# Layer 0's selective scan: dt and u are spread over the partitions by transfers from DRAM instead of by TensorE's products

## The chip, the cores and the metric

The kernel runs on one core of one Trainium2 chip. The metric is the device time of one execution, in microseconds (us); less is better. Of the kernel before there are three runs, with a median of 7452.86 us (7450.63 to 7460.66), and one execution under the hardware profiler.

The core has five engines with instruction streams of their own: TensorE (PE, matrix products, with PEld for its weight loads), VectorE (DVE), ScalarE (ACT), GpSimd (POOL) and SyncE (SP), which here only issues DMA transfers. They meet through semaphores. SBUF is the working memory of 128 partitions; PSUM, of eight banks of 512 float32 columns in each partition, takes TensorE's results, and DVE and ACT can read and write it. Transfers are carried out by 16 DMA engines.

## What is computed

Four residual layers work on x of 8 images, 128 channels and 64x64 pixels, float32. The change is in layer 0, in a selective state-space scan over the 4096 pixels of an image, with 128 inner channels d and N = 16 states n:

```python
dbc = xc @ xproj_w
dt = softplus(dbc[..., :R] @ dt_w + dt_b)
Bm = dbc[..., R:R + N]
Cm = dbc[..., R + N:]
A = -exp(A_log)
dA = exp(dt[..., None] * A)
dBx = dt[..., None] * Bm[:, :, None, :] * xc[..., None]
# step: h = dA_t * h + dBx_t ;  y_t = sum over n of h * C_t
```

So each of 128 x 16 pairs (d, n) has a recurrence of its own along the pixels. The decay is exp(dt[d] A[d, n]), the input u[d] B[n] with u = dt xc, and the output is weighed by C[n] and summed over n. Layer 0 further has a group norm, a small projection t, a layer norm, a convolution of three taps along the pixels, gates, and a 3x3 convolution of the other 64 channels. Layer 1 is a recurrence over image rows and then columns, of convolutions with nine taps; layers 2 and 3 follow.

## The kernel before

**Tiles and steps.** `layer0` works through 32 chunks of 1024 pixels, four an image; a chunk is two halves h of T = 512 pixels. The 2048 recurrences of a half are 16 rows of 128, since 128 partitions hold 8 channels with 16 states each. A *step* takes two of these rows: 8 steps a half, 16 a chunk, 512 in all. `where(i)` gives the chunk, the half, and (r, j0): the step's rows are the channels 32 j + 8 r to 32 j + 8 r + 7 for j = j0 and j0 + 1.

**What a step does.** `step_dt` (through `spread`, L571 to L580) multiplies 32 rows of dt by a mask `m_dt` that holds A at (d, n) and zeros elsewhere: PE so copies each channel to its 16 partitions and scales it by A, into `dt_ps` in PSUM. `step_decay` (L592) takes the exponential of both rows in one ACT instruction, into `da`. `step_u` does the same as `step_dt` for u with the mask `m_u` of ones, into `u_ps`. `step_scan` multiplies `u_ps` by B on DVE, in place (L599), and runs two scans, one for each row, into `hb` (L610); `carry` gives the start values. `step_carry` and `step_weigh` on POOL keep the last column (L616) and multiply `hb` by C (L621). Every second step, `round_sum` sums over n with a mask on PE (L629), into `ps_y`.

**What a chunk does once.** `plan_chunk` puts some 30 pieces of work at ticks relative to t0 = 16 c: load and norm of x, the product for t (L362) and its variance, products for x and z (`xs_product`, L392; `z_product`, L404), the softplus for dt in pieces from `v_product` to `v_sum`, and after the scan `y_gate`, `y_mul`, the 3x3 convolution (L484), `y_product` and the stores. `v_sum` (L439 to L441) makes dt and u with three POOL operations a half, into SBUF. `bc_product` writes B and C to a small DRAM tile `bcd`, and `bc_spread` (L457) loads them back, eight transfers a half of 16 partitions each, so that each partition has its n's row of B and C in one tile `bc`.

**What sets the order.** The order is written out by hand: the loop at L645 to L662 issues, for tick i, the scan of step i, layer 1's addition, u of step i + 1, dt of step i + 2, the sum of i - 3, the decay of i + 2, carry and weighing of i - 1, then the chunk pieces of tick i, and last layer 1's products. Each engine, SyncE among them, executes its own part of that order strictly in sequence; semaphore waits follow from the tiles. All of layer 0's transfers are issued by SyncE.

**Layer 1 inside layer 0.** From tick 294 on `Layer1First` adds one row of layer 1's recurrence to each tick, for the first four images: 18 matmul instructions (L739) at the end of a tick, and one DVE operation (L747) at the next. It needs 252 ticks and goes on for 34 after the last scan. Its PSUM bank is the second of two `u_ps` pairs, which layer 0 gives up at tick 280.

**PSUM of layer 0:** two `u_ps` of two banks, `dt_ps` of two banks, one bank for `ps_y` and one (`ps_g`) for all products of the chunk pieces.

Of the kernel before, what the change touches and what calls it, by code (L numbers as in the profile page):

```python
# [10 lines left out]
F32 = mybir.dt.float32  # L11
I32 = mybir.dt.int32
AF = mybir.ActivationFunctionType
ALU = mybir.AluOpType
# [3 lines left out]
P = 128  # L18
# [16 lines left out]
def conv_preact_kernel(ctx: ExitStack, tc: tile.TileContext, a: dict, out: bass.AP):  # L35
# [31 lines left out]
    bcd = [dram.tile([P // 2, T], F32, name=f"bcd{i}") for i in range(2)]  # L67
# [12 lines left out]
    layer0(tc, a, ident, gmat, x_in, x1d, bcd, norm1, Layer1First(tc, a, w1, x1d, norm1, X))  # L80
# [67 lines left out]
def layer0(tc, a, ident, gmat, x_in, x1d, bcd, norm1, layer1):  # L148
# [5 lines left out]
    nc = tc.nc  # L154
    CH = 2 * T
    CR = CH // W
    NCK = HW // CH
    with ExitStack() as ctx:
# [3 lines left out]

        pu = ctx.enter_context(tc.tile_pool(name="l0u", bufs=1, space=PSUM))
        pdt = ctx.enter_context(tc.tile_pool(name="l0dt", bufs=1, space=PSUM))
        py = ctx.enter_context(tc.tile_pool(name="l0y", bufs=1, space=PSUM))
        pg = ctx.enter_context(tc.tile_pool(name="l0g", bufs=1, space=PSUM))
# [25 lines left out]
        a_neg = load("a_neg", [DI, N], (ALL, a["A_log"]))  # L192
# [4 lines left out]
        with tc.manual_schedule():  # L197
# [5 lines left out]
            def ps_g(name):  # L203
                return pg.tile([P, T], F32, tag="g", name=name)
# [47 lines left out]
            quad = wp.tile([P, 32], F32, name="quad")  # L252
            nc.vector.tensor_copy(quad, ident[:, 0:32])
            for j in range(1, 4):
                nc.vector.tensor_add(quad, quad, ident[:, 32 * j : 32 * j + 32])
            m_u = wp.tile([P, 4, 8, N], F32, name="m_u")
            nc.vector.tensor_copy(
                m_u, quad.rearrange("p (r d) -> p r d", d=8).unsqueeze(3).to_broadcast([P, 4, 8, N])
            )
            m_dt = wp.tile([P, 4, 8, N], F32, name="m_dt")  # L260
            nc.vector.tensor_mul(
                m_dt, m_u, a_neg.unsqueeze(1).unsqueeze(1).to_broadcast([P, 4, 8, N])
            )
# [70 lines left out]

            def plan_chunk(c):
# [50 lines left out]
                def xs_product(h):  # L386
                    q, sl = s["q"], (LO, HI)[h]
                    if h == 0:
                        s["xz"] = w2.tile([DI, 6, T], F32, name="xz", bufs=1)
                    ps = ps_g("ps_x")  # L390
                    for k in range(KC):
                        nc.tensor.matmul(  # L392
                            ps, lhsT=w_k[sl, k, :], rhs=q[sl, k : k + T], start=(k == 0), stop=(k == KC - 1)
                        )
                    edge = KC - 1 if g == 0 and h == 0 else 0
                    x = s["xz"][:, h]
                    nc.scalar.activation(x[:, edge:], ps[:, edge:], AF.Identity, bias=b_xc[:, 2:3])
                    for i in range(edge):
                        nc.scalar.activation(x[:, i : i + 1], ps[:, i : i + 1], AF.Identity, bias=b_xc[:, i : i + 1])

                def z_product(h):
                    q, sl = s["q"], (LO, HI)[h]
                    ps = ps_g("ps_z")
                    nc.tensor.matmul(ps, lhsT=in_w[sl, DI:], rhs=q[sl, KC - 1 :], start=True, stop=True)  # L404
                    nc.scalar.activation(s["xz"][:, 2 + h], ps, AF.Identity, bias=in_b[:, 1:2])
# [29 lines left out]
                def v_sum(h):  # L435
                    dt = s["dt", h] = w2.tile([DI, T], F32, name=f"dt{h}", bufs=1)
                    u = s["u", h] = w2.tile([DI, T], F32, name=f"u{h}", bufs=1)
                    w = s["w"][:, h]
                    nc.gpsimd.tensor_add(w, w, s["e"][:, h])  # L439
                    nc.gpsimd.tensor_add(dt, w, s["rv"][:, h])  # L440
                    nc.gpsimd.tensor_mul(u, dt, s["xc"][:, h])  # L441
# [12 lines left out]
                def bc_spread(h):  # L454
                    bc = s["bc", h] = w2.tile([P, 2, T], F32, name="bc")
                    for d in range(8):
                        nc.sync.dma_start(  # L457
                            bc[16 * d : 16 * d + 16],
                            bcd[c % 2][32 * h : 32 * h + 32, :].rearrange("(i n) t -> n i t", n=N),
                        )  # L460
# [72 lines left out]
                at(t0 - 25, t_product)  # L533
                at(t0 - 24, t_var)
# [3 lines left out]
                at(t0 - 21, t_norm)  # L538
                at(t0 - 19, t_edge)
                for h in range(2):  # L540
                    at(t0 - 16 + h, also(xs_product, h))
                    at(t0 - 14 + h, also(z_product, h))
                    at(t0 - 11 + h, also(v_product, h))
                    at(t0 - 6 + 4 * h, also(v_sum, h))
                    at(t0 - 6 + 8 * h, also(bc_spread, h))
                    at(t0 + 10 + 8 * h, also(y_gate, h))
                    at(t0 + 11 + 8 * h, also(y_mul, h))
                at(t0 - 13, silu)
                at(t0 - 9, bc_product)
                at(t0 - 10, v_exp)  # L550
                at(t0 - 9, v_round)
                at(t0 - 8, v_rest)
                at(t0 - 7, v_log)
# [17 lines left out]
            def spread(i, ps, mask, src):  # L571
                c, h, r, j0 = where(i)
                for j in (0, 1):
                    q = slice(32 * (j0 + j), 32 * (j0 + j) + 32)
                    nc.tensor.matmul(  # L575
                        ps[:, j, :],
                        lhsT=mask[q, r].rearrange("p d n -> p (d n)"),
                        rhs=S[c][src, h][q, :],
                        start=True, stop=True,
                    )  # L580

            def step_u(i):
                steps[i]["bc"] = u_ps[0 if i > shared else i % 2]
                spread(i, steps[i]["bc"], m_u, "u")

            def step_dt(i):
                steps[i] = {"dt": pdt.tile([P, 2, T], F32, name="dt_ps")}
                spread(i, steps[i]["dt"], m_dt, "dt")

            def step_decay(i):  # L590
                da = steps[i]["da"] = w2.tile([P, 2, T], F32, name="da", bufs=3)
                nc.scalar.activation(da, steps[i]["dt"], AF.Exp)  # L592

            def step_scan(i):
                c, h, r, j0 = where(i)
                s, st = S[c], steps[i]
                if r == 0 and j0 == 0:
                    s["carry", h] = w2.tile([P, 4, 4], F32, name="carry")
                nc.vector.tensor_mul(  # L599
                    st["bc"], st["bc"], s["bc", h][:, 0].unsqueeze(1).to_broadcast([P, 2, T])  # L600
                )
                hb = st["hb"] = w2.tile([P, 2, T], F32, name="hb", bufs=4)
                for j in (0, 1):
                    if h:
                        start = s["carry", 0][:, r, j0 + j : j0 + j + 1]
                    elif c % NCK:
                        start = S[c - 1]["carry", 1][:, r, j0 + j : j0 + j + 1]
                    else:
                        start = 0.0
                    nc.vector.tensor_tensor_scan(  # L610
                        hb[:, j, :], st["da"][:, j, :], st["bc"][:, j, :], start, ALU.mult, ALU.add
                    )
# [5 lines left out]
            def step_weigh(i):  # L618
                c, h, r, j0 = where(i)
                hb = steps[i]["hb"]  # L620
                nc.gpsimd.tensor_mul(hb, hb, S[c]["bc", h][:, 1].unsqueeze(1).to_broadcast([P, 2, T]))  # L621
# [15 lines left out]

            shared = n_steps // 2 + 24
            u_ps = [pu.tile([P, 2, T], F32, name=f"u_ps{i}") for i in range(2)]
            layer1.begin(16 * NCK, shared, u_ps[1])  # L640
# [4 lines left out]
            for i in range(min(events), n_steps + 60):  # L645
                if 0 <= i < n_steps:
                    step_scan(i)
                layer1.add(i)
                if 0 <= i + 1 < n_steps:
                    step_u(i + 1)  # L650
                if 0 <= i + 2 < n_steps:
                    step_dt(i + 2)
                if i % 2 and 0 <= i - 3 < n_steps:
                    round_sum(i - 3)
                if 0 <= i + 2 < n_steps:
                    step_decay(i + 2)
                if 0 <= i - 1 < n_steps:
                    step_carry(i - 1)
                    step_weigh(i - 1)
                for what in events.pop(i, ()):  # L660
                    what()
                layer1.products(i)  # L662
# [9 lines left out]
class Layer1First:  # L672
# [5 lines left out]
    def begin(self, batch, first, bank):  # L678

        ps = bank[:, 0, 0 : W * NB2].rearrange("p (w b) -> p w b", b=NB2)  # L680
        self.steps = propagate(self.tc, self.a, self.wp, ps, self.X)
        self.batch, self.first = batch, first + 14
# [601 lines left out]
def layouts(i):  # L1284
# [20 lines left out]
        "A_log": i["L0_conv_A_log"],  # L1305
# [34 lines left out]
```

## Time and profile before

| | before |
|---|---|
| median of three runs | 7452.86 us |
| the profiled execution | 7436.8 us |
| its span | 7435.1 us |
| PE busy | 5633.9 us, 76% |
| DVE busy | 4822.2 us, 65% |
| POOL busy | 4120.9 us, 55% |
| ACT busy | 3349.0 us, 45% |
| moved by DMA | 935.09 MB, mean 126 GB/s |
| first scan; first product of layer 1; last scan | 96.9; 1445.6; 2955.8 us |

In the page's groups a line has the source line, the engine and the operation, what is written and read, the count, then busy time and mean duration of one, and last the idle time of the engine just before with what ended most of it. In a table by stretch a row has the stretch and its length, then for each engine the busy time and, in brackets, the number of instructions, the granted share of TensorE's clock, the mean busy share of the 16 DMA engines, and what they moved. A line of a timeline has start and length, the engine and the source line. fp32 products appear as two PE instructions each.

### The profile page before, as it was taken

To read this page: it belongs to the slowest core of one execution; us is meant where nothing else is said; L and a number is where in the kernel's file an instruction comes from. 1 tells how busy PE (TensorE), PEld (TensorE's weight loads), DVE (VectorE), ACT (ScalarE), POOL (GpSimd) and SP (SyncE) were. 2 spreads that over 40 slices of the span, in tenths; PEclk is the share of its full clock that TensorE was granted. 3 is DMA by queue.
4 is the path that set the end of the run, shared out by engine and by line. 5 is a ranking of instruction groups with operands and counts; after the bars stand their busy time and mean duration, and the time that the engine had idled before them with its cause. 6 is when DMAs were issued, how large, how long until landed. Compare 5 with 4: busy or idle time off the path is not lost.

```text
span 7435.1 us, 79753 instructions
## 1 busy us (share of the span) xinstructions
PE 5633.9 (76%) x25130; PEld 3374.0 (45%) x25130; DVE 4822.2 (65%) x6334; ACT 3349.0 (45%) x7610; POOL 4120.9 (55%) x3773
## 2 busy tenths in 40 slices
PE   6888888899999999779898988984556565554330
PEld 1222222255556556647676767762333333333220
DVE  4988889666666666230366666758767676776665
ACT  3555655433333332020255555554556565565552
POOL 3878778545545454000255555555666666666664
PEclk9888888799999999989999999996777677776665
DMA  1111111101100100130356666667677666666667
GB/s 57 43 58 54 57 56 53 42 29 34 32 30 30 31 20 18 59 124 24 96 180 188 189 183 180 192 187 243 211 217 219 208 212 209 211 212 201 187 182 272
DMA packets 360134, 935.09 MB, mean 126 GB/s; under 512 B 64168, under 2 KB 99248, under 8 KB 357664
## 3 DMA queue, kind: packets, MB, share of 16 engines
q0 software_dynamic: 184320, 604.13, 26.7%
q1 hardware_dynamic: 170784, 309.09, 12.8%
q10 hardware_dynamic: 4608, 16.78, 0.6%
q8 instruction: 200, 3.28, 0.2%
q14 instruction: 222, 1.82, 0.1%
HBM read 804.35 MB, written 125.40 MB: 125 GB/s over the span
## 4 chain that ended last, share of the span: by engine, by line
PE 56%; ACT 11%; issue 9%; DVE 9%; another core or an unknown queue 7%; DMA 4%; POOL 4%; SPq 0%; POOLq 0%; DVEq 0%; ACTq 0%
PE u_ps L739 13%; PE ps_l L739 11%; ACT X L1184 6%; PE u_ps L575 5%; PE ps_o L1227 5%; PE ps_c L484 3%; PE ps_t L900 3%; PE ps_y L629 3%; PE ps_s L1209 2%; PE ps_x L392 2%; DVE hb L610 2%; POOL hb L621 2%; PE ps_off L1017 2%; PE ps_t L926 1%
## 5 line engine op out<-in xcount | busy, mean ns | idle before, releaser
L1173 POOL DMA_INDIRECT X<-table,idx x1386 | 1317.9, 951 | 717.0 <-issue 276.6
L1173 POOL DMA_INDIRECT got<-table,idx x918 | 885.1, 964 | 1291.2 <-DVE idx L1078 529.6
L621 POOL TENSOR_TENSOR hb<-hb,bc 128x1024 f32<-128x1024 f32 x512 | 1207.1, 2358 | 47.0 <-POOL carry L616 4.5
L610 DVE TENSOR_TENSOR_SCAN hb<-da,carry,u_ps 128x512 f32<-128x512 f32 x896 | 1097.8, 1267 | 76.4 <-PE ps_y L629 19.8
L592 ACT ACTIVATE da<-dt_ps 128x1024 f32<-128x1024 f32 x512 | 524.8, 1025 | 1284.2 <-PE dt_ps L575 1087.4
L1184 ACT ACTIVATE X<-X,wgt 128x128 f32<-128x128 f32 x2772 | 867.5, 396 | 41.5 <-issue 37.7
L1227 PE MATMUL ps_o<-samp,dcn_w 128*128 128x256 f32 x2304 | 711.8, 455 | 182.9 <-issue 95.8
L1219 ACT COPY samp<-ps_s 128x384 f32<-128x384 f32 x768 | 362.9, 473 | 1043.9 <-remote 563.0
L575 PE MATMUL u_ps<-u,m_u 32*128 32x512 f32 x2048 | 652.3, 716 | 131.2 <-DVE hb L610 130.5
L599 DVE TENSOR_TENSOR u_ps<-u_ps,bc 128x1024 f32<-128x1024 f32 x512 | 625.8, 1222 | 191.2 <-PE dt_ps L575 173.9
L1209 PE MATMUL ps_s<-ident,X 128*128 128x128 f32 x1386 | 306.4, 344 | 576.2 <-ACT samp L1219 287.0
L575 PE MATMUL dt_ps<-dt,m_dt 32*128 32x512 f32 x2048 | 664.0, 728 | 31.5 <-ACT da L592 25.7
L1227 PEld LDWEIGHTS ps_o<-samp,dcn_w 128*128 128x128 f32 x2304 | 507.3, 231 | 309.4 <-issue 128.6
L747 DVE SCALAR_TENSOR_TENSOR X<-ps_l,X 128x256 f32<-128x256 f32 x252 | 106.6, 423 | 734.5 <-PE ps_l L739 553.6
L1200 DVE TENSOR_TENSOR prod<-prod,X 128x384 f32<-128x384 f32 x462 | 260.8, 565 | 480.0 <-ACT X L1184 320.5
L1184 ACT ACTIVATE got<-got,wgt 128x128 f32<-128x128 f32 x1836 | 570.3, 393 | 1.1 <-issue 1.1
L1209 PEld LDWEIGHTS ps_s<-ident,X 128*128 128x128 f32 x1386 | 206.1, 176 | 708.9 <-ACT samp L1219 330.5
L616 POOL COPY carry<-hb 128x2 f32<-128x2 f32 x512 | 111.4, 218 | 735.0 <-DVE hb L610 678.8
L1189 DVE TENSOR_TENSOR prod<-X,prod 128x768 f32<-128x768 f32 x462 | 444.5, 962 | 46.2 <-ACT prod L1156 27.6
L747 DVE SCALAR_TENSOR_TENSOR X<-u_ps,X 128x256 f32<-128x256 f32 x252 | 106.9, 424 | 562.7 <-PE u_ps L739 560.4
L900 PE MATMUL ps_t<-xn,w 128*128 128x512 f32 (+4 forms) x688 | 344.8, 656 | 66.5 <-issue 23.0
L575 PEld LDWEIGHTS u_ps<-u,m_u 32*128 32x128 f32 x2048 | 169.6, 202 | 483.6 <-DVE hb L610 282.2
(227 smaller groups left out, 10644.6 us busy)
## 6 DMA issues: line engine op xcount, KB each, us to landing
bc<-bcd SPq DMA_DIRECT2D x512, 64.0 KB
table<-tok SPq DMA_DIRECT2D x128, 256.0 KB
x<-x1d SPq DMA_DIRECT2D x96, 256.0 KB
X<-table,idx POOLq DMA_INDIRECT x1386
x<-x2d SPq DMA_DIRECT2D x48, 384.0 KB
x3h<-x3d SPq DMA_DIRECT2D x16, 1056.0 KB
x_st<-in_x SPq DMA_DIRECT2D x64, 256.0 KB
x_o<-in_x SPq DMA_DIRECT2D x64, 256.0 KB
```

The source lines that it names most:

```text
L575: nc.tensor.matmul(ps[:, j, :], lhsT=mask[q, r].rearrange("p d n -> p (d n)"), rhs=S[c][src, h][q, :], start=True, stop=True,)
L592: nc.scalar.activation(da, steps[i]["dt"], AF.Exp)
L599: nc.vector.tensor_mul(st["bc"], st["bc"], s["bc", h][:, 0].unsqueeze(1).to_broadcast([P, 2, T]))
L610: nc.vector.tensor_tensor_scan(hb[:, j, :], st["da"][:, j, :], st["bc"][:, j, :], start, ALU.mult, ALU.add)
L621: nc.gpsimd.tensor_mul(hb, hb, S[c]["bc", h][:, 1].unsqueeze(1).to_broadcast([P, 2, T]))
L739: nc.tensor.matmul(ps[:, c0:c1, :], lhsT=w[:, k, :], rhs=v[:, prev, c0 + k - PAD : c1 + k - PAD, :], start=(k == PAD), stop=(k == K - 1),)
L900: nc.tensor.matmul(ps[:, o0 - a0 : o1 - a0, :], lhsT=self.w1[:, k, :], rhs=S["xn", g][:, i0 + o0 : i0 + o1, :], start=(k == 2), stop=(k == 4),
L1173: nc.gpsimd.indirect_dma_start(out=got[:, k, :, :].rearrange("p q c -> p (q c)"), out_offset=None, in_=tab, in_offset=bass.IndirectOffsetO ...
L1184: nc.scalar.activation(got[:, k, q, :], got[:, k, q, :], AF.Identity, scale=wgt[:, t, k0 + k, q : q + 1])
L1189: nc.vector.tensor_mul(prod, got[:, :, 0:2, :], w.unsqueeze(3).to_broadcast([P, G3, 2, C]))
L1209: nc.tensor.transpose(ps[:, k, :], got[:, k, 0, :], self.ident)
L1227: nc.tensor.matmul(ps, lhsT=self.dcn_w[:, k, :], rhs=samp[:, k - k0, :], start=(k == 0), stop=(k == KK - 1))
```

## The change

dt and u no longer go through PE.

- `v_sum` stores both to DRAM with the new `keep`, eight transfers a chunk, of 64 rows by 512 columns each. In DRAM the rows are ordered (a, r, d, j), so that the two rows j of a channel that belong to one step are next to each other.
- `step_dt` and `step_u` are now one transfer each: 8 channels of 2 x 512 floats, each read for 16 partitions (`to_broadcast`), straight into `da` and `hb`. They are issued four and three steps ahead; `da` has five buffers instead of three and `hb` six instead of four.
- A is no longer in a mask. `a_neg` is reshaped to 16 columns by 128 partitions, and `step_decay` gives a column as `scale` to ACT: two instructions of 128x512, in place in SBUF, instead of one of 128x1024 from PSUM.
- `bc_spread` is one transfer for B and one for C a half, with a leading broadcast of 8. B goes to a tile that shares the buffer `tcen`, and `b_copy` on ACT moves it to PSUM. The product u B reads `hb` and B and writes a PSUM tile of its own (`ps_ub`); the scans write `hb` as before.
- In PSUM now: two banks for `ps_ub`, two for B, one for `ps_y`, one for layer 1, two for the chunk products. With two of these, `xs_product` and `z_product` do both halves in one tick, with the halves' instructions in turn, and `v_product` does both at one tick.
- The pieces of the chunk before the scan move one tick earlier in part (`t_product` to `t_edge`, and `v_product` to `v_sum`). Layer 1 begins at tick 294 as before.

```diff
@@ layer0: PSUM pools
         pu = ctx.enter_context(tc.tile_pool(name="l0u", bufs=1, space=PSUM))
-        pdt = ctx.enter_context(tc.tile_pool(name="l0dt", bufs=1, space=PSUM))
+        pb = ctx.enter_context(tc.tile_pool(name="l0b", bufs=2, space=PSUM))
         py = ctx.enter_context(tc.tile_pool(name="l0y", bufs=1, space=PSUM))
-        pg = ctx.enter_context(tc.tile_pool(name="l0g", bufs=1, space=PSUM))
+        pl = ctx.enter_context(tc.tile_pool(name="l01", bufs=1, space=PSUM))
+        pg = ctx.enter_context(tc.tile_pool(name="l0g", bufs=2, space=PSUM))
...
-        a_neg = load("a_neg", [DI, N], (ALL, a["A_log"]))
+        a_neg = load("a_neg", [P, 4, 4], (ALL, a["A_log"]))
...
+            def keep(d, t):
+                d = d.rearrange("(a r d j) t -> a j (r d) t", a=2, r=4, j=2)
+                for a in range(2):
+                    nc.sync.dma_start(d[a], t[64 * a : 64 * a + 64])
...
-                def xs_product(h):
...
+                def xs_product():
+                    s["xz"] = w2.tile([DI, 6, T], F32, name="xz", bufs=1)
+                    pss = [ps_g("ps_x") for _ in range(2)]
                     for k in range(KC):
+                        for ps, sl in zip(pss, (LO, HI)):
+                            nc.tensor.matmul(
+                                ps, lhsT=w_k[sl, k, :], rhs=s["q"][sl, k : k + T],
+                                start=(k == 0), stop=(k == KC - 1),
+                            )
...
                 def v_sum(h):
-                    dt = s["dt", h] = w2.tile([DI, T], F32, name=f"dt{h}", bufs=1)
-                    u = s["u", h] = w2.tile([DI, T], F32, name=f"u{h}", bufs=1)
-                    w = s["w"][:, h]
+                    w, dt = s["w"][:, h], s["rv"][:, h]
                     nc.gpsimd.tensor_add(w, w, s["e"][:, h])
-                    nc.gpsimd.tensor_add(dt, w, s["rv"][:, h])
-                    nc.gpsimd.tensor_mul(u, dt, s["xc"][:, h])
+                    nc.gpsimd.tensor_add(dt, w, dt)
+                    keep(dtu[c % 2][h][0], dt)
+                    nc.gpsimd.tensor_mul(w, dt, s["xc"][:, h])
+                    keep(dtu[c % 2][h][1], w)
...
                 def bc_spread(h):
-                    bc = s["bc", h] = w2.tile([P, 2, T], F32, name="bc")
-                    for d in range(8):
-                        nc.sync.dma_start(
-                            bc[16 * d : 16 * d + 16],
-                            bcd[c % 2][32 * h : 32 * h + 32, :].rearrange("(i n) t -> n i t", n=N),
-                        )
+                    b_in = s["b_in"] = w2.tile([P, T], F32, tag="tcen", name="b_in", bufs=1)
+                    s["C", h] = w2.tile([P, T], F32, name="C")
+                    for i, t in enumerate((b_in, s["C", h])):
+                        at = 32 * h + N * i
+                        nc.sync.dma_start(t, bcd[c % 2][at : at + N, :].unsqueeze(0).to_broadcast([8, N, T]))
+
+                def b_copy(h):
+                    s["B", h] = pb.tile([P, T], F32, name="ps_b")
+                    nc.scalar.copy(s["B", h], s["b_in"])
...
-            def spread(i, ps, mask, src):
+            def spread(i, k, t):
                 c, h, r, j0 = where(i)
+                src = dtu[c % 2][h][k].rearrange("(a r d j) t -> a r d (j t)", a=2, r=4, j=2)[j0 // 2, r]
+                nc.sync.dma_start(t.rearrange("p j t -> p (j t)"), src.unsqueeze(1).to_broadcast([8, N, 2 * T]))
+
+            def step_dt(i):
+                steps[i] = {"da": w2.tile([P, 2, T], F32, name="da", bufs=5)}
+                spread(i, 0, steps[i]["da"])
+
+            def step_u(i):
+                steps[i]["hb"] = w2.tile([P, 2, T], F32, name="hb", bufs=6)
+                spread(i, 1, steps[i]["hb"])
+
+            def step_decay(i):
+                _, _, r, j0 = where(i)
+                da = steps[i]["da"]
                 for j in (0, 1):
-                    q = slice(32 * (j0 + j), 32 * (j0 + j) + 32)
-                    nc.tensor.matmul(
-                        ps[:, j, :],
-                        lhsT=mask[q, r].rearrange("p d n -> p (d n)"),
-                        rhs=S[c][src, h][q, :],
-                        start=True, stop=True,
-                    )
...
+                    nc.scalar.activation(da[:, j], da[:, j], AF.Exp, scale=a_neg[:, r, j0 + j : j0 + j + 1])
...
-                nc.vector.tensor_mul(
-                    st["bc"], st["bc"], s["bc", h][:, 0].unsqueeze(1).to_broadcast([P, 2, T])
-                )
-                hb = st["hb"] = w2.tile([P, 2, T], F32, name="hb", bufs=4)
+                hb = st["hb"]
+                ub = pu.tile([P, 2, T], F32, name="ps_ub")
+                nc.vector.tensor_mul(ub, hb, s["B", h].unsqueeze(1).to_broadcast([P, 2, T]))
...
@@ the loop over ticks
-                if 0 <= i + 1 < n_steps:
-                    step_u(i + 1)
-                if 0 <= i + 2 < n_steps:
-                    step_dt(i + 2)
+                if 0 <= i + 4 < n_steps:
+                    step_dt(i + 4)
                 if i % 2 and 0 <= i - 3 < n_steps:
                     round_sum(i - 3)
+                if 0 <= i + 3 < n_steps:
+                    step_u(i + 3)
                 if 0 <= i + 2 < n_steps:
                     step_decay(i + 2)
```

## The prediction

> **What bounds the kernel now.** I read the page, then busy time by stretch, then groups, chain and timeline inside the stretches, last the DMA. All the change touches runs from the first scan (93 us) to the last (2958 us): 512 steps. Layer 1's first products are at 1445 us, step 294, so there are two stages. Busy time by stretch:
>
> ```profile
> core 0: us, PE busy (x) PEld busy (x) DVE busy (x) ACT busy (x) POOL busy (x), PEclk, DMA share, GB/s
> 93.00:1445.00 1352.00, 1127.85 (x4925) 294.08 (x4924) 1169.75 (x1082) 721.71 (x847) 1050.80 (x815) 0.83 0.17 52
> 1445.00:2960.00 1515.00, 1497.30 (x7490) 904.12 (x7491) 967.48 (x988) 483.42 (x564) 764.58 (x594) 0.99 0.09 28
> 2960.00:3127.00 167.00, 145.89 (x658) 118.41 (x658) 20.57 (x47) 7.08 (x9) 7.56 (x7) 1.00 0.04 14
> ```
>
> Stage 1 takes 1352/294 = 4.60 us a step; DVE is busy 1170/294 = 3.98 of them and PE 3.84, each waiting for the other in turn. Stage 2 takes 1515/218 = 6.95 us a step and is PE's, at 99%. DMA is idle five sixths of the time. Work of a step, from the page's groups:
>
> ```profile
> L621 POOL TENSOR_TENSOR hb<-hb,bc 128x1024 f32<-128x1024 f32 x512 | 1207.1, 2358 | 47.0 <-POOL carry L616 4.5
> L610 DVE TENSOR_TENSOR_SCAN hb<-da,carry,u_ps 128x512 f32<-128x512 f32 x896 | 1097.8, 1267 | 76.4 <-PE ps_y L629 19.8
> L592 ACT ACTIVATE da<-dt_ps 128x1024 f32<-128x1024 f32 x512 | 524.8, 1025 | 1284.2 <-PE dt_ps L575 1087.4
> L599 DVE TENSOR_TENSOR u_ps<-u_ps,bc 128x1024 f32<-128x1024 f32 x512 | 625.8, 1222 | 191.2 <-PE dt_ps L575 173.9
> ```
>
> The chain of stage 2, in order of time, shows what the removed products cost there: they run in pairs, u beside dt, from 2202.46 to 2203.53, that is 1.07 us a step.
>
> ```profile
> 2202.46 0.63 PE u_ps L575 x2
> 2203.09 0.01 PE dt_ps L575 x2
> 2203.10 0.41 PE u_ps L575 x2
> 2203.51 0.01 PE dt_ps L575 x2
> 2203.53 1.00 PE ps_y L629 x8
> 2204.52 2.77 PE ps_x L392 x6
> ```
>
> The DMA answer for 300 to 1300 us (14 chunks): SyncE's queue, then the issues that the change replaces.
>
> ```profile
> q1 hardware_dynamic: 30016, 53.93, 17.2%
> ...
> bc<-bcd SPq DMA_DIRECT2D x224, 64.0 KB
> ```
>
> And SyncE's timeline in layer 2, where two stores of 67 rows (L869) are followed by three of 64 rows:
>
> ```profile
> 3692.83 0.68 SPq L869 DMA_DIRECT2D table<-zero  x2
> 3693.55 7.88 SPq L871 DMA_DIRECT2D table<-zero  x3
> ```
>
> Issuing those three takes 7.88 us, where three ordinary issues take about 1.3. The packet records behind it show the 67-row stores' 2048-byte packets one after another, one each 80 ns: a single engine works on them.
>
> [...] packets of 2048 bytes last 86 ns in the store of 128 partitions (L513) and 151 in that of 64 (L452). [...]
>
> **The change, part by part.**
>
> PE loses eight product records a step, 1.07 us in stage 2 and some 2.0 in stage 1 (1010.56 to 1012.58 us, at a lower clock). `xs_product` and `z_product` now alternate halves of the rows, as u and dt did, so a second half costs about nothing: 2.77 + 1.05 = 3.8 us a chunk, 0.24 a step. PE would need 6.95 - 1.07 - 0.24 = 5.64 us a step in stage 2.
>
> ACT: `step_decay` becomes two exponentials of 128x512. The nearest row is L305's from SBUF, 626 ns: 1.25 us for 1.02. `b_copy` adds two of about 0.58 a chunk. ACT was busy 2.45 us a step and becomes 2.75; the period hides it, and it would cost 0.3 a step without cover. DVE and POOL do the same work: 3.98 and 3.57 us. The removed masks and the reshaped A are before the loop.
>
> DMA, of a chunk of 16 steps. `step_dt` and `step_u`: 32 transfers of 512 KB, 16.8 MB where the whole queue carried 53.93/14 = 3.9. The source is 8 rows x 16 repeats x 4096 bytes[...]. Packets of 4096 bytes last 159 ns (the median in the records, at the end of the kernel). 32 x 16 x 159 ns = 81.4 us[...]. `bc_spread`: four of 8 x 16 rows[...]: 4 x 16 x 84 ns = 5.4. `keep`: eight stores of 64 rows into (2, 32) rows[...]: 8 x 32 packets[...]: 151 ns, 38.7 us; 86 ns, 22.0[...]. What stays: 17.2% of 1000 us over 14 chunks is 12.3 us, less L457's 32 packets an engine at 0.101, 3.2: 9.1.
>
> Engine 0: 81.4 + 5.4 + 9.1 + 22.0 to 38.7 = 118 to 135 us a chunk, 7.4 to 8.4 us a step. That is more than either stage's period: DMA becomes the bound of both, and what PE gives up is worth nothing. [...] (151/86 = 1.76) [...] (81.4 + 5.4) x 1.76 + 9.1 = 162 us, 10.1 a step. [...] I take the middle, 8.75[...].
>
> SyncE: dt of step i+4 waits for the scan of i-1 (five `da`), u of i+3 for `round_sum(i-3)` (six `hb`). Behind them stand `keep`, `bc_spread`, image loads and output stores. When scan i-1 has run, u of i+1 and i+2 and dt of i+2 and i+3 are still queued, over 10 us of transfers, so these waits don't empty the engines. `keep` must land before its half's first dt, three steps later, some 26 us: enough, unless stores queue behind more. `b_in` shares `tcen` with `t_norm`, a step earlier: hidden. At the start `keep` comes ahead of the first scan: +15 us.
>
> Sum: 512 x 8.75 = 4480, before 1352 + 1515 = 2867: +1613, +15. Span 7435.1 + 1628 = 9063, the execution 1.7 more; the median of the runs (7452.86) stands 16 above the profiled execution (7436.8), so 9080 us.
>
> **The rivals.**
>
> All sixteen engines serve the transfers[...]. Then 32 x 8 x 159 ns + 2.7 + 5 + 9.1 is 57.5 us a chunk, 3.6 a step, hidden. Stage 1 falls to DVE's 3.98 and some 0.17 of gaps, 4.15: -132; stage 2 to 5.64: -286. 7453 - 418 = 7035. For it: the idle DMA above, and that the waits of DVE and ACT are all for PE. Against it: the 67 rows. This decides for faster where the busiest engine needs less than 2867/512 = 5.6 us a step.
>
> The spreads use sixteen but `keep` two: 40.7 + 2.7 + 38.7 + 9.1 = 91 us, 5.7 a step; stage 1 +323, stage 2 -272: 7500. [...]
>
> [...] 10.1 a step: 5171 - 2867 + 15 = +2319, 9770. It is the forecast's own upper end.
>
> **How the numbers follow.** Eight engines, 7.4 to 10.1 us a step: 0.83, with its own range 8390 (512 x 7.4 - 2867 + 15 on 7453) to 9770. Sixteen throughout: 0.10. Only `keep` narrow: 0.04. Slower still[...]: 0.03. The three runs span 0.13%, so under 0.2% nothing can be told. Range 8200 to 10000: it leaves out the faster cases, most of the slowest, and a few in a hundred of the forecast by a cheaper `keep`. Faster 0.11, same 0.01, slower 0.88.
>
> **What would show it.** The DMA share near one half in both stages (eight full engines of sixteen), never near 0.8; stages of nearly equal step time, so stage 1 longer by far more than stage 2; DVE and ACT waiting for `da` and `hb` by DMA; PE busy far under 99% in stage 2; scan, weighing and product at 1.27, 2.36 and 1.22 us. It is wrong if the share passes 0.6 at a step of 5.6 us or less, if DVE's product slows, or if SyncE's waits, not the packets, fill the gaps.

## The result, and the profile after

The changed kernel took 8477.57 us (median of four runs, 8469.99 to 8495.37) where the kernel before took 7456.76 beside it (7450.63 to 7467.47): a ratio of 1.137, 95% interval 1.135 to 1.139. The forecast was 9080 with a range of 8200 to 10000, so the direction and the range were right and the value was 600 us too high. The profiled span is 8468.3 us, against 7435.1.

Busy time by stretch, with the columns of the table shown for before: stage 1 (first scan to layer 1's first product), stage 2 (to the last scan), and the rest of layer 1's first half.

```profile
98.00:2316.00 2218.00, 997.15 (x2546) 229.59 (x2548) 1198.39 (x1080) 816.91 (x1175) 1047.96 (x808) 0.55 0.50 180
2316.00:3957.00 1641.00, 1326.94 (x5741) 883.69 (x5738) 950.53 (x988) 553.64 (x806) 767.78 (x594) 0.90 0.48 173
3957.00:4135.00 178.00, 151.45 (x680) 122.12 (x679) 27.58 (x56) 7.07 (x9) 10.10 (x9) 0.98 0.06 20
```

Both stages now run at one pace: from scan to scan 7.54 us a step in stage 1 (before 4.57) and 7.56 in stage 2 (6.98). Stage 1 is 873 us longer, stage 2 126, and the first scan comes 2 us later: 1001 of the span's 1033 us. The other 32 lie behind the last scan, in code that was not touched; in the pair of traces taken later on one chip they are absent (there the last scan is 996 us later and the span 994 longer). None of PE, DVE, ACT and POOL is full any more: PE is busy for 45% of stage 1 and 81% of stage 2, DVE for 54 and 58. The DMA share stands at one half in both stages, which is what eight engines of sixteen, nearly full, would look like.

The page's groups, for the same four pieces of a step as before, in the order POOL, DVE, ACT, DVE:

```profile
L624 POOL TENSOR_TENSOR hb<-hb,C 128x1024 f32<-128x1024 f32 x512 | 1208.4, 2360 | 41.3 <-POOL carry L619 0.6
L613 DVE TENSOR_TENSOR_SCAN hb<-da,carry,ps_ub 128x512 f32<-128x512 f32 x896 | 1098.3, 1268 | 81.8 <-DVE ps_ub L605 58.1
L596 ACT ACTIVATE da<-da,a_neg 128x512 f32<-128x512 f32 x1024 | 681.2, 712 | 2129.0 <-DMA da<-dtd 2045.8
L605 DVE TENSOR_TENSOR ps_ub<-hb,ps_b 128x1024 f32<-128x1024 f32 x512 | 628.8, 1228 | 1450.5 <-DMA hb<-ud 1448.6
```

The weighing (2360 ns for 2358), the scan (1268 for 1267) and DVE's product (1228 for 1222) cost what they did. What changed is the last column: ACT stands 2046 us for `da` by DMA, and DVE 1449 us for `hb` by DMA, where both waited for PE before. The waits of 300 to 2300 us say the same; the columns are the total, the number of waits and the longest, in us:

```profile
ACT da L596 <- DMA da<-dtd: 969.3, 188, 15.1
DVE ps_ub L605 <- DMA hb<-ud: 848.3, 246, 14.1
```

SyncE's queue and the two new transfers, from the page's parts on DMA:

```profile
q1 hardware_dynamic: 319776, 879.52, 29.4%
...
da<-dtd SPq DMA_DIRECT2D x512, 512.0 KB
hb<-ud SPq DMA_DIRECT2D x512, 512.0 KB
```

And SyncE's timeline for one stretch of stage 1:

```profile
1249.00 3.62 SPq L331 DMA_DIRECT2D dtd<-xz  x2
1252.72 5.12 SPq L331 DMA_DIRECT2D ud<-xz  x2
1257.96 5.73 SPq L582 DMA_DIRECT2D da<-dtd  x1
1263.79 1.18 SPq L582 DMA_DIRECT2D hb<-ud  x1
```

An issue that takes some 0.53 us in a run below takes up to 5.73 here, and SyncE is issuing for 69% of stage 1. Two readings fit: the engines that serve the queue are short, or SyncE itself has become the bound. The experiments start there. (The chain that ended last can't be used: its traced pieces lie behind layer 1.)

### The profile page after: what moved, and what is told of

It is laid out like the page before. It is cut to its first block, busy times and chain, and to the rows that moved or that the text cites. A ratio compares the mean times of both kernels' runs of the same rounds, so it can differ in the third digit from the quotient of the medians.

```text
span 8468.3 us, 75234 instructions
## 1 busy us (share of the span) xinstructions
PE 5330.0 (63%) x21034; PEld 3291.6 (39%) x21034; DVE 4830.3 (57%) x6328; ACT 3510.8 (41%) x8186; POOL 4120.5 (49%) x3773
## 5 line engine op out<-in xcount | busy, mean ns | idle before, releaser
L596 ACT ACTIVATE da<-da,a_neg 128x512 f32<-128x512 f32 x1024 | 681.2, 712 | 2129.0 <-DMA da<-dtd 2045.8
L605 DVE TENSOR_TENSOR ps_ub<-hb,ps_b 128x1024 f32<-128x1024 f32 x512 | 628.8, 1228 | 1450.5 <-DMA hb<-ud 1448.6
L624 POOL TENSOR_TENSOR hb<-hb,C 128x1024 f32<-128x1024 f32 x512 | 1208.4, 2360 | 41.3 <-POOL carry L619 0.6
L613 DVE TENSOR_TENSOR_SCAN hb<-da,carry,ps_ub 128x512 f32<-128x512 f32 x896 | 1098.3, 1268 | 81.8 <-DVE ps_ub L605 58.1
L632 PE MATMUL ps_y<-hb,m_y 128*32 128x512 f32 x2048 | 451.6, 810 | 593.2 <-POOL carry L619 392.1
L739 PE MATMUL ps_l<-X,w_right 128*128 128x256 f32 x2268 | 540.0, 396 | 125.6 <-DVE X L747 83.5
L739 PE MATMUL ps_l<-X,w_left 128*128 128x256 f32 x2268 | 537.1, 394 | 121.0 <-DVE X L747 81.8
L739 PE MATMUL ps_l<-X,w_up 128*128 128x256 f32 x2268 | 537.5, 394 | 101.8 <-DVE X L747 74.8
L739 PE MATMUL ps_l<-X,w_down 128*128 128x256 f32 x2268 | 530.5, 390 | 78.9 <-DVE X L747 77.4
L739 PEld LDWEIGHTS ps_l<-X,w_right 128*128 128x128 f32 x2268 | 448.9, 202 | 234.5 <-DVE X L747 117.7
```

The lines of the kernel that those rows point to most:

```text
L596: nc.scalar.activation(da[:, j], da[:, j], AF.Exp, scale=a_neg[:, r, j0 + j : j0 + j + 1])
L605: nc.vector.tensor_mul(ub, hb, s["B", h].unsqueeze(1).to_broadcast([P, 2, T]))
L613: nc.vector.tensor_tensor_scan(hb[:, j, :], st["da"][:, j, :], ub[:, j, :], start, ALU.mult, ALU.add)
L624: nc.gpsimd.tensor_mul(hb, hb, S[c]["C", h].unsqueeze(1).to_broadcast([P, 2, T]))
L632: nc.tensor.matmul(S[c]["ps_y", h][32 * j : 32 * j + 32, :], lhsT=m_y[:, r, :], rhs=steps[i + j // 2]["hb"][:, j % 2, :], start=(r == 0), ...
L739: nc.tensor.matmul(ps[:, c0:c1, :], lhsT=w[:, k, :], rhs=v[:, prev, c0 + k - PAD : c1 + k - PAD, :], start=(k == PAD), stop=(k == K - 1),)
```

## The experiments

They ran on several chips. On most of them the unchanged layers behind layer 1's first half are faster: the kernel before takes 7000 us there, but in the trace taken there its two stages are the same. So ratios and stages are compared, not totals; the totals expected of the first three edits are on the scale of the first chip, where the kernel before takes 7457. "A step" is the time from scan to scan; packet times are means over the records of the 4096-byte packets in stage 1. Each ratio has several runs behind it, each step time one trace.

**The two kernels on one chip.**

> The changed kernel again, on the chip of the other experiments, for its ratio and its stages there. All theories: stages of 7.5 and 7.6 us a step as in the first run, some 1020 us over the kernel before (7003 here), so a ratio near 1.145.

> The kernel before, for a trace on the chip of the experiments. Stages of 4.57 and 6.98 us a step as on the first chip; what follows layer 1's first half near 3890 us, as in the other runs on this chip, instead of 4312.

Ratio 1.144 (1.142 to 1.146); steps of 7.53 and 7.55 us after, 4.57 and 6.98 before. What follows layer 1's first half takes 3881 and 3884 us. So the whole loss is in the two stages.

**n outermost.** The partitions of a step are ordered (n, d), so the source of a spread is 16 repeats of 8 rows; B and C are spread in the same order. Bytes and number of issues stay; only what stands outermost changes.

```diff
- src.unsqueeze(1).to_broadcast([8, N, 2 * T])
+ src.unsqueeze(0).to_broadcast([N, 8, 2 * T])
```

> Partitions in the order (n, d) instead of (d, n), so that the broadcast source of da, hb, B and C has 16 rows outermost. Theory 1, the busiest DMA engine sets the step: these transfers run on 16 engines instead of 8, engine 0 has 43 + 9 + 22 to 39 us a chunk, 4.7 to 5.7 us a step; stage 1 near 4.9 us a step, stage 2 at PE's 5.6 to 5.8, time 7200 to 7450. Theory 2, SyncE's issues and waits set the step, not the engines: the same number of issues, so 8300 to 8500, no change. Theory 3, only the stores of dt and u on two engines bind: 8000 to 8400, since they stay.

Ratio 1.038 (1.037 to 1.040), steps of 6.02 and 6.23 us. That is the direction of theory 1, but not the 4.9 and 5.6 to 5.8 us a step that it named.

**`keep` over sixteen engines.** Its eight stores of (2, 32) rows a chunk become sixteen of 32 rows.

```diff
- nc.sync.dma_start(d[a], t[64 * a : 64 * a + 64])
+ for j in range(2):
+     nc.sync.dma_start(d[a, j], t[64 * a + 32 * j : 64 * a + 32 * j + 32])
```

> Each store of 64 rows is cut in two of 32 rows with 32 outermost, so that it runs on 16 engines; the spreads stay on 8. Theory 1: engine 0 loses the stores, some 20 us of 120.6 a chunk, and is as loaded as engines 1 to 7: 6.0 to 6.5 us a step, 7700 to 7950. Theory 2: eight more issues a chunk, 0.5 us each: 8500 to 8650. Theory 3: down to the periods of the compute engines, under 7400.

Ratio 1.172 (1.169 to 1.175), steps of 7.82 and 7.91 us. In the two stages that is 164 us more than the changed kernel, so some 8640 on the first chip: the number of theory 2, at the edge of its range, and far from theory 1. But it is not theory 2's cause: SyncE issues for 53% of stage 1 where it did for 69%, and the packets below show full engines.

**Both edits.**

> Both edits. Theory 1: at most 60 us a chunk on any engine, 3.7 us a step, hidden: stage 1 at DVE's 4.15 us a step, stage 2 at PE's 5.64, 7035 (6980 to 7200), faster than the kernel before. Theory 2: 8500 or more. Theory 3: as with the stores alone.

Ratio 1.011 (1.010 to 1.013), steps of 5.52 and 6.04 us, far from the 4.15 and 5.64 of theory 1. The stretch from 300 to 1300 us, in the run with n outermost, with `keep` alone and with both:

```profile
300.00:1300.00 1000.00, 554.92 (x1454) 129.61 (x1451) 678.59 (x610) 466.26 (x671) 597.95 (x463) 0.57 0.89 226
```

```profile
300.00:1300.00 1000.00, 446.61 (x1118) 101.79 (x1120) 512.95 (x464) 343.06 (x497) 454.55 (x351) 0.53 0.56 170
```

```profile
300.00:1300.00 1000.00, 592.13 (x1586) 136.56 (x1588) 739.50 (x673) 499.49 (x722) 653.76 (x506) 0.58 0.99 245
```

The last two columns settle the first question. With n outermost the share goes from 0.50 to 0.89 with the same count of issues, so SyncE's issuing was not the bound: eight engines it was. The packet records say so too, if one counts how many packets are in flight at once in stage 1. In the changed kernel it is eight or nine for 71% of the time, exactly two for 12%, and practically never fewer than two. With n outermost it is sixteen or more for 80%, and still two for 11%; with `keep` alone eight or nine for 78%, and two for 0.5%; with both edits sixteen or more for 93%. So the changed kernel's spreads run on eight engines, and the stores of `keep` on two that never rest.

A spread's issue falls from a mean of 1.2 to 1.4 us to 0.6 to 0.7 with n outermost and to 0.53 or 0.54 with both edits. That is not because the engines have room, for with both they are fuller than ever; the long issues went with the transfers on eight engines, and why was not tried.

The two columns also open a second question. When `keep` no longer loads two engines alone, nothing is gained: all eight are now full (0.56 of sixteen, where a half is theirs and the rest is other work; eight packets or more are in flight for 96% of stage 1), but their 4096-byte packets take 208 ns where the changed kernel has 175. And with both edits all sixteen are full at 0.99, but with packets of 271 ns instead of 159. So 8 x 32 packets of 271 ns, by estimate, cost an engine 69 us a chunk, not the 41 of the forecast's rival. Two causes were considered: the order in which the partitions of SBUF are written when the source is 16 x 8 rows, or the reading: the same 8 rows of DRAM are read sixteen times each, with sixteen packets in flight. No trace had shown either.

**Doubled rows.** Each row of dt and u is stored twice, so the source of a spread is again 16 x 8 rows, but of sixteen different rows, each read eight times. (`keep` is in stores of 32 rows; B and C still come as 8 x 16 rows, as in the changed kernel.)

```diff
- src = ...rearrange("(a r d j) t -> a r d (j t)", ...)
- ...src.unsqueeze(1).to_broadcast([8, N, 2 * T])
+ src = ...rearrange("(a r d s j) t -> a r (d s) (j t)", ..., s=2, ...)
+ ...src.unsqueeze(1).to_broadcast([16, 8, 2 * T])
```

> The changed kernel, but keep writes each row of dt and u twice, side by side, by eight stores of 32 rows, so that a spread reads 16 rows, eight times each, instead of 8 rows sixteen times[...]. [...] packets of 4096 bytes near 270 ns, an engine 69 us a chunk by them and 20 by the rest, 5.5 to 5.7 and 6.0 to 6.2 us a step, ratio 1.01 to 1.03. Theory of the rows (16 engines that read one row of DRAM at once hinder each other): packets near 165 ns, some 60 us a chunk, hidden; 4.15 and 5.64 us a step, ratio near 0.94.

Ratio 1.062 (1.060 to 1.065), packets of 274 ns and not 165, with half as many reads of a row: that a row is read by many at once is not the cause. The steps, 6.42 and 6.50 us, are longer than expected, by 14 us a chunk in stage 1 against the run with both edits. The doubled stores are a part of that: by estimate 32 more packets of 2048 bytes an engine and chunk at 137 ns, 4.4 us. Another part is idle engines: the DMA share is 0.93 only, with sixteen packets or more in flight for 79% of the time. B and C, with a source of 8 x 16 rows as the changed kernel's spreads had (eight or nine packets in flight), could leave such gaps, but that was not tried apart.

**128 rows, in blocks and plain.** Two runs with both edits read 128 different rows of x instead: one in the order (n, d), 16 x 8 rows that don't merge, one as 128 plain rows.

```diff
+ src = x_in[c // NCK][:, 2 * T * (c % NCK) : ...]
+ nc.sync.dma_start(t..., src.rearrange("(d n) t -> n d t", n=N))   # in blocks
+ nc.sync.dma_start(t..., src)                                      # plain
```

> Both edits (n outermost, keep over 16 engines) as in the run with both, but a spread reads 128 different rows of x in the order n, d (16 x 8 rows that don't merge), so [...] no row is read twice; A is 0 for finite sums. The output is not the reference's: the recurrence runs on x and without decay; work and bytes are the same. [...] packets near 270 ns as in the run with both, 5.5 and 6.0 us a step, ratio near 1.01. Theory that 8 or 16 rows of DRAM read many times at once are what is slow: packets near 190 ns as with the plain 128 rows, 4.5 and 6.0 us a step, ratio near 0.966.

> Both edits (n outermost, keep over 16 engines), but a spread reads 128 rows of x instead of 8 rows of dt or u, so its sides are both 128 rows and no row is read twice; A is 0 for finite sums. The output is not the reference's: the recurrence runs on x and without decay; work, bytes and packets are the same. [...] packets near 160 to 180 ns, engines some 60 us a chunk, hidden: 4.15 and 5.64 us a step, ratio near 0.94. Theory of the rows: the same here, so it is told apart by the run with doubled rows. A limit of DRAM or of all engines together near 245 GB/s: packets stay near 270 ns, 5.5 and 6.0 us a step, ratio near 1.01.

In blocks: ratio 1.007 (1.005 to 1.009), 269 ns, steps of 5.53 and 6.02 us. Plain: ratio 0.966 (0.964 to 0.968), 192 ns, median 159, steps of 4.50 and 6.00. The same bytes from the same rows; the stretch from 300 to 1300 us, blocks first:

```profile
300.00:1300.00 1000.00, 590.32 (x1588) 137.30 (x1584) 739.96 (x674) 501.05 (x724) 654.18 (x507) 0.59 0.99 246
```

```profile
300.00:1300.00 1000.00, 656.63 (x1922) 157.36 (x1918) 895.92 (x817) 616.04 (x891) 793.22 (x614) 0.64 0.90 301
```

The engines' full time moves 246 GB/s in blocks; plain, 90% of it moves 301. So neither a limit of DRAM nor the repeated rows set the 245 GB/s, but the form of the source: 16 x 8 rows or 128 plain ones. What was read differed among the three runs with 16 x 8 rows, which all have 269 to 274 ns; that the writing of the partitions is the likelier part is the author's estimate from these three. The records name neither the engine nor the partitions of a packet, so why it takes 269 ns in blocks and 192 plain was not shown.

**DMA only where PE is short.** A spread that can't be plain without storing every row sixteen times stays at 5.5 us a step, which hurts in stage 1 alone, where the kernel before needs 4.57. The first version keeps dt as PE's product in chunks 0 to 17, with u by DMA.

```diff
+ if 16 * CUT <= i + 3 < n_steps: step_dt(i + 3)          # by DMA, CUT = 18
+ if 0 <= i + 2 < 16 * CUT: product_dt(i + 2)             # by PE
- at(t0 - 2 + 8 * h, also(b_copy, h))                     # two ps_b
+ at(t0 - 1 + 8 * h, also(b_copy, h))                     # one ps_b
```

> Both edits, but in the first 18 chunks dt stays PE's product (its two matmuls read different rows, so they can run side by side), and only u comes by DMA; from chunk 18 on, where layer 1 runs on PE, both come by DMA. Room for it: one buffer of B in PSUM instead of two, four da and five hb, loads one step later. Expected[...]: half the spreads in stage 1, 16 x 8 x 190 to 270 ns = 24 to 35 us on an engine a chunk, hidden; DVE sets stage 1 at 4.2 to 4.4 us a step; stage 2 as with both, 6.0; 294 x 4.3 + 217 x 6.04 = 2575 where the kernel before has 2858: near 6715, ratio 0.96. Rival, that the step's own order and not DMA or PE keeps stage 1 at 4.57: near 6790, ratio 0.971. Rival, that fewer buffers and later loads leave DVE and ACT waiting for the transfers: stage 1 over 4.8, ratio 0.98 or more.

Ratio 0.999 (0.998 to 1.000), steps of 5.21 and 6.09 us: in the range of the last rival. DVE's waits from 300 to 1300 us point to the buffer taken from B, which cost more than the later loads.

```profile
DVE ps_ub L627 <- ACT ps_b L477: 114.5, 12, 10.1
DVE ps_ub L627 <- DMA hb<-ud: 73.3, 41, 6.0
```

Once a chunk DVE stands some 9.5 us for the copy of B, 0.6 us a step. PE did not gain either: it holds half of the old products, but is granted 0.62 of its clock in that stretch where before has 0.83, and a product record of dt lasts 924 ns where before has 776. The stretch in the kernel before, then in this run:

```profile
300.00:1300.00 1000.00, 840.90 (x3752) 220.42 (x3752) 891.19 (x826) 545.67 (x641) 805.68 (x624) 0.83 0.17 55
```

```profile
300.00:1300.00 1000.00, 870.79 (x2444) 204.36 (x2444) 766.16 (x700) 527.65 (x769) 680.79 (x526) 0.62 0.59 153
```

**Both by PE in stage 1, both by DMA in stage 2.** Chunks 0 to 17 work as before (B from SBUF, nothing kept), and the banks of `u_ps` and `dt_ps` serve B, the product with B and layer 1 from chunk 18 on.

```diff
+ if i < 16 * CUT: ub = u = u_ps[i % 2]
+ else: hb = u = st["hb"]; ub = u_ps[0]; B = dt_ps[:, h]
```

> Where layer 1 leaves PE free (chunks 0 to 17) dt and u are PE's products as before, B comes from SBUF and nothing is kept in DRAM; from chunk 18 on both come by DMA with both edits (n outermost, keep over 16 engines), B in PSUM. The masks hold no A, so the decay is two exponentials with a scale throughout. Expected, if DMA was the loss of stage 1 alone and PE's 1 us a step the gain of stage 2: stage 1 near the kernel before, 4.6 us a step, stage 2 6.05; 294 x 4.6 + 217 x 6.05 = 2665 where before has 2858, near 6810, ratio 0.972. Rival: what held stage 1 at 5.2 us in the run with mixed transport was not its transport but the decay in two halves behind one buffer of dt in PSUM; then stage 1 is again near 5.2 and the ratio near 1.0.

Ratio 1.000 (0.999 to 1.001), steps of 4.98 and 6.45 us. Stage 1 lies between the two expectations; why stage 2 takes 6.45 and not 6.05 was not followed. The next run puts A back into the mask, for one exponential in stage 1 (and has three buffers of `da` there instead of four).

```diff
- for j in (0, 1): activation(da[:, j], dt_ps[:, j], AF.Exp, scale=a_neg[...])
+ activation(da, dt_ps, AF.Exp)
```

> As the run with DMA in stage 2 alone, but in stage 1 the mask holds A again, so the decay is one exponential of 128x1024 out of PSUM as before. If the two halves of the decay cost stage 1 its 0.4 us a step (4.98 against 4.57): stage 1 returns to 4.55 to 4.65, stage 2 stays at 6.46; 294 x 4.6 + 217 x 6.46 = 2754 where before has 2860, a ratio near 0.986. If they did not, and the order of the products or the third buffer of da did: stage 1 stays near 5.0, ratio near 1.0.

Ratio 0.999 (0.998 to 1.000), steps of 4.93 and 6.46 us: the two changes together bring 0.05 us, not 0.4. Its waits from 300 to 1300 us name other work, which the change's schedule had moved. There two PSUM buffers for the products of the chunk pieces had covered it, and here there is one (`ps_v` is `v_product`'s use of it, and `res` L542 is ACT's reading of `y_product` out of it):

```profile
DVE u_ps L664 <- PE dt_ps L621: 95.0, 44, 8.2
POOL dtu L469 <- PE dt_ps L621: 60.0, 13, 13.6
PE ps_v L448 <- ACT res L542: 59.6, 13, 4.6
```

The last run moves two of these pieces back by a tick: `v_product` of the second half, in all chunks, and `v_sum`, in stage 1 alone.

```diff
- at(t0 - 12, also(v_product, h)); at(t0 - 7 + 4 * h, also(v_sum, h))
+ at(t0 - 12 + h, also(v_product, h)); at(t0 - 7 + (c < CUT) + 4 * h, also(v_sum, h))
```

> As the last run, with two pieces of a chunk's work back at the ticks where one g buffer in PSUM and the tiles of dt and u allow them without a wait: the second half's v_product a tick after the first's, v_sum a tick later in stage 1. In the last run PE stood 59.6 + 71.1 us of 1000 behind ACT's reads of that buffer, and POOL 60.0 us behind PE's products of dt. If that is what kept stage 1 at 4.93: 4.6 us a step, stage 2 6.4; 294 x 4.6 + 217 x 6.4 = 2741 where before has 2860, ratio near 0.984. If the first waits are other work's shadow: 4.9, ratio near 1.0.

Ratio 0.986 (0.984 to 0.988), steps of 4.69 and 6.30 us: 1.4% faster than the kernel before. Stages 1 and 2, 300 to 1300 and 1800 to 2800 us:

```profile
300.00:1300.00 1000.00, 804.36 (x3640) 211.92 (x3644) 874.37 (x790) 522.82 (x616) 773.75 (x604) 0.84 0.17 50
1800.00:2800.00 1000.00, 919.68 (x4212) 618.75 (x4210) 690.99 (x714) 411.34 (x595) 561.05 (x439) 0.97 0.85 208
```

In stage 1 DVE is the busiest engine again (87%), at 0.84 of PE's clock and with DMA idle for five sixths; in stage 2 the transfers run at a share of 0.85 under PE's 92%. The same waits from 300 to 1300 us:

```profile
DVE u_ps L664 <- PE dt_ps L621: 53.9, 28, 4.2
POOL dtu L469 <- PE dt_ps L621: 20.7, 7, 4.8
PE ps_v L448 <- ACT res L542: 58.3, 13, 4.6
```

The wait of `ps_v` for `res` stayed, while POOL's and DVE's for the products of dt fell, DVE's by 0.2 us a step. That points to the tick of `v_sum` for stage 1's 0.23 us, but the two ticks were not moved apart. In stage 2, where only `v_product` moved, the step fell as well, from 6.46 to 6.30.

## Why the prediction was right, and where its size was off

- **Eight engines, and the bound moves to DMA.** Right. How many engines serve each new transfer was the author's estimate, for which the trace of before had one example, the stores of 67 rows with their packets one after another, 80 ns apart; the packets in flight in the changed kernel then showed eight for the spreads and two for `keep`. A share near one half (0.50 and 0.48), equal steps, waits for `da` and `hb` by DMA and PE far under 99% in stage 2 (81%) were named beforehand. What shows the cause is the run with n outermost: same bytes, same issues, sixteen engines, and 10 points of the ratio come back.
- **The time of a step: 8.75 us taken, 7.54 measured.** This is the term that was mis-sized. The steps were to cost 1613 us more than before and cost 999; these 614 us are the whole of the error, as the smaller terms nearly cancel. The 7.4 of the low end, with packets of 159 ns, was nearly the answer, and the middle between it and 10.1 was the error. The 10.1 stretches packets by 1.76, the ratio of the 151 and 86 ns of two stores out of SBUF; that packets into SBUF would stretch so was the author's estimate, and no trace of before showed it. The 4096-byte packets averaged 175 ns, between 159 and 280 (159 x 1.76), so 13% of the way and not half; in the later runs it was 40% of the way with `keep` alone (208 ns) and over 90% with sixteen engines (271). What stretches them was not shown. So the low end came out for no reason that the forecast had, and that part was luck.
- **The busiest engine sets the chunk.** Right. A step of 7.54 us is 120.6 us a chunk, in the 118 to 135 that the forecast gave its engine 0 (the records name no engine). The six of the eight that don't serve `keep` have, by estimate, 32 x 16 x 175 ns = 89.6, and 15 of smaller work, some 105, which leaves them idle for 13% of a chunk; exactly two packets were in flight for 12% of stage 1. But that was a bound with little behind it: relieved of the stores, the packets went 40% of the way to 280 ns and the chunk took 125 us. Why they got longer there was not tried.
- **"All sixteen engines", 7035 us.** As a rival it was rightly thought unlikely, but its working was wrong: it charged 159 ns for a packet, and sixteen engines in blocks take 271. The transfers then need 69 us a chunk for spreads alone, stage 1 is still theirs at 5.52 us, and the ratio of the run with both edits is 1.011 where the rival's 7035 us are 0.944.
- **PE's saving in stage 2.** The step's PE work was forecast at 5.64 us; in the run with plain rows PE is 94.9% busy (1800 to 2800 us) in steps of 6.00, which is 5.69. The price was right. The other 0.3 us are idle time of PE, which the forecast left out; PE and DVE wait for each other around layer 1 there (from 1700 to 2700 us DVE 243.8 us for PE's products, PE's weight loads 81.1 us for DVE's `X`). DVE's 4.15 us in stage 1 came out as 4.50, with a DMA share of 0.90 beside it.
- **ACT.** An exponential with a scale for each partition takes 712 ns, not 626: 1.42 us a step for the 1.25 of the forecast, 0.4 above the kernel before. The period hid it.
- **SyncE.** That its waits don't empty the busiest engines holds: in the changed kernel two packets or more are in flight practically always. Its long issues were not foreseen; they went with the transfers on eight engines. "+15 us at the start" was 2.
- **DVE and POOL keep their times.** Right, as the groups show: the weighing 2360 ns for 2358, the product 1228 for 1222. Whether B's place in PSUM has a part in that was not tried, so only the equal times are shown.

## What to carry to other kernels

Before a broadcast goes to DMA, write down the form of each transfer's source, and find in a trace how many of its packets are in flight and how long they last: here 8 x 16 rows had eight or nine in flight, 16 x 8 rows sixteen or more and moved 246 GB/s, and 128 plain rows moved 301. A change that relieves an engine belongs in the stretch where that engine ends last; here the transfers on eight engines cost 873 us where PE alone was not the bound, and 126 even where it was, and a version on sixteen engines that used them only there came out 1.4% ahead. And a forecast with an interval for an unknown factor should not take its middle without a reason for the middle.

## What the runs showed of the hardware

- 4096-byte packets into SBUF: median 159 ns with 128 plain rows, a mean of 192; a mean of 269 to 274 with three different sources of 16 x 8 rows (8 rows read sixteen times each, 16 rows read eight times each, 128 different rows).
- The same packets with a source of 8 x 16 rows: 175 ns in the changed kernel (eight or nine packets in flight for 71% of stage 1, exactly two for 12%), and 208 with `keep` in stores of 32 rows (eight or nine in flight for 78%).
- An issue of a spread on SyncE took 0.53 or 0.54 us on average with both edits, at a DMA share of 0.99, and in the changed kernel's stage 1, at a share of 0.50, 1.2 us for `da` and 1.4 for `hb`, 5.73 at most. The long issues came with the transfers on eight engines; they were not what bound the kernel.
- PE's granted clock, from 300 to 1300 us: 0.54 after (1168 records, PE busy 46%), 0.62 in the run that took half of the products from PE (2444 records, 87%), 0.83 before (3752 records, 84%); in stage 2 before it was 0.99 (99%). Of the first three, the order is that of the number of product records and not that of the busy share, but the run with plain rows doesn't quite keep to it (0.64 with 1922 records, 66%). What sets the clock was not tried.
